# A graph attention kernel with residual norm: order of the norm pass, place of the key products, place of the list check, and an addition on GpSimd

## The chip, the core and the metric

The kernel runs on one core of one Trainium2 chip. The core has five engines with instruction queues of their own: TensorE (matrix products, PE in the profile, with its weight loads as PEld), VectorE (DVE), ScalarE (ACT), GpSimd (POOL) and SyncE (SP), which here only issues DMA transfers. They work side by side and wait for each other through semaphores. Each queue is worked off in order, so an instruction that waits holds everything behind it on its engine. The metric is the device time of one execution, in microseconds (us); lower is better.

## What is computed

A batch of 8 graphs with 2048 nodes and 64 features goes through two graph attention layers that share one adjacency matrix, then through two normalisations with a residual. Cut to what matters:

```python
h = jnp.einsum('bnc,hdc->bhnd', x, Wh)                 # four heads
out_h = _gat_layer(h, mask, bh)                         # softmax over neighbours of h.h, times h
z = leaky_relu(concat_heads(out_h), 0.2)
h2 = jnp.einsum('bnk,dk->bnd', z, Wo)
out2 = _gat_layer(h2, mask, bo)                         # the second layer, one head
z2 = leaky_relu(out2, 0.2)
out = (z2 - mean(z2)) * rsqrt(var(z2) + 1e-5) * gamma + beta
return _layernorm(x + out)                              # a second normalisation
```

`mask` is the adjacency with the diagonal set. The graph is sparse: node i and node j are joined with a probability that falls with both numbers, so the first nodes have many neighbours and the others few.

## The kernel before

The 2048 nodes are split into 56 hubs, which are treated densely, and 166 sets of 12 nodes. For each set the kernel makes a list of at most 128 nodes that any of its 12 members is joined to, gathers those rows from a table in device memory by an indirect DMA, and does attention of the 12 members against the 128 rows. The program is written in the order in which each engine is to work; nothing is reordered later.

**Lists.** The adjacency is read in pieces of 480 KB (`load_adj`, L646). SyncE issues the transfer into one of three buffers `raw`, GpSimd turns it into 0 and 1 in a tile `a` (L657) and sets the diagonal (L664). There are five buffers for `a`. `make_keys` (L689) multiplies the pieces with powers of two on TensorE (L700, tile `pk`) and packs the result with the node number into `keys` on VectorE (L685). In the first layer it has one PSUM tile, `T`, so its second half waits until VectorE has read its first half. `pick` (L710) returns a list of small VectorE jobs that take the largest keys out, eight at a time (`max` L722, `match_replace` L724), then merge them, turn them on TensorE (`slots`, L746) and build the indices and the masks. The lists come in two rounds. Round 0 (60 sets) is ready before the first layer begins. Of round 1 (106 sets) `make_keys` is called four times, k3 = 0 to 3; the first two calls lie before the first layer, the last two in it.

**First layer** (L967): a loop over 83 pairs of sets in a software pipeline. Step i issues two gathers for pair i+5, turns the rows of pair i+3 (L508), makes scores of pair i+1 (L808), masks them on VectorE (L813), takes the exponential on ScalarE (L820), multiplies by the values (L833) and divides by the sums on VectorE (`invert`, L840 and L841). Pair i goes through the head weights, and older pairs through the second projection (L867, L870) into the table of the second layer. At the end of the step come one of six pieces of the hubs (`slow`, in steps 0 to 5: turn back, heads, table, for each half of the graphs), up to two adjacency pieces (`more`), and list jobs: `some(1)` ahead of `invert`, `some(2)` behind `more`, then `make_keys` as soon as the pieces that it needs have been issued. Nine pieces are left at step 0, so these calls fall into steps 2 and 4. The 58 jobs of round 1 begin at step 5, and gathers that need round 1 begin at step 25.

**Second layer** (L1302): a loop over u, with four sets a step. A step issues gathers for step u+5 (L779, with 24 row buffers), scores for u+1 (`scores2`: L1075, exponential L1078), the value products for u (`values2`, L1103), turns of the rows for u+3 (L508, copied at L1283), the turn back of the exponentials for u+1 (L1086) and their product with the mask on VectorE (L1090). Two steps share a PSUM tile `o`, with one buffer: the even step begins it and the odd step ends it.

**Norm passes.** Behind each odd step stands the normalisation of those eight sets, number v = (u-1)/2, 21 in all, and one pass for the hubs. A pass is cut into jobs that `spread` (L1265) deals out over the following steps, and `work_on` (L1269) runs the jobs of a step at its end. Their names: `first` divides by the sums and frees `o` (L1129, L1131); `act` is the leaky slope (L1136); `mean` a sum (L1140); `centre` subtracts the mean and has ScalarE square the result (L1145, L1147); `var` sums the squares (L1152); `again` scales, multiplies by gamma, adds beta and adds the input rows `xr` (L1156, L1160, L1161, L1162); `end` scales once more and stores. `spread` appends, so the jobs of older passes in a step come before `first` of the new one. In an odd step these are either three `var` or one `again`. Every fourth step ends with a square root on ScalarE for all variances (L1274) and a reciprocal (L1275). The rows `xr` are loaded by SyncE, eight transfers a pass (L1190), and the results leave in eight transfers (L1197).

**The end.** After the last step the lists and the sums are checked against limits (L1329 to L1343): eleven small VectorE operations, a product on TensorE, and a flag that is written to device memory. Every engine then loads the flag and skips a general version of the kernel.

Of the kernel before, what the change touches and what calls it, by code (L numbers as in the profile page):

```python
# [359 lines left out]
def fast_kernel(ctx: ExitStack, tc: tile.TileContext, x, adj, Wh, bh, Wo, bo, gamma, beta, out, flag):  # L360
# [534 lines left out]
    def some(n):  # L895
        for _ in range(n):
            if picks:
                picks.pop(0)()
# [68 lines left out]
    for i in range(-3, NG + 3):  # L967
        sp = one(f"s{i}", "S")
        if 0 <= i - 3 < NG:
            second_rows(i - 3, sp[:GM, 1, 384:512])  # L970
        if 0 <= i - 2 < NG:
            second_maps(i - 2, sp[:, 0, 384:384 + GM])
        if 0 <= i + 1 < NG:
            scores(i + 1, sp)
            weigh(i + 1, sp)
        if 0 <= i < NG:
            turn_values(i, op)
            keep_values(i, op)
# [12 lines left out]
        if 0 <= i + 3 < NG:  # L991
            tp = one(f"t{i + 3}", "T")
            for j in range(2):
                turn(tp[:, j, :], rows[1, 2 * (i + 3) + j])
        if i < NG:
            cat = one(f"cat{i}", "C")
        if 0 <= i + 3 < NG + NG % 2:
            columns(i + 3, cat)
        if 0 <= i < NG:
            project(held.pop(("ot", i)), cat, GM)  # L1000
        if 0 <= i + 1 < NG:
            op = one(f"o{i + 1}", "O")
            values(i + 1, op)

        if 0 <= i - 2 < NG:
            nc.vector.tensor_copy(own[:, (i - 2) * GM:(i - 1) * GM], sp[:, 0, 384:384 + GM])
        if 0 <= i - 3 < NG:
            keep_rows(i - 3, sp[:GM, 1, 384:512])
        if 0 <= i - 1 < NG:
            leak(held["z", i - 1])  # L1010
        if 0 <= i + 3 < NG:
            t = held["T", 1, i + 3] = work.tile([P, 2, 512], F32, tag="xTg", name=f"xTg{i + 3}", bufs=3)
            nc.scalar.copy(t, tp)  # L1013
        if 0 <= i < NG:
            held["z", i] = leaky(cat, GM, f"z{i}")
        if 0 <= i + 3 < NG + NG % 2:
            keep_columns(i + 3, cat)
        if i >= 0:
            some(1)
        if 0 <= i + 1 < NG:  # L1020
            invert(i + 1, op)

        if i >= 0:
            if slow:
                slow.pop(0)()
            more(2)
            some(2)
            done = all(t // 3 > k3 for r, t, m in pieces)
            if k3 < nk and done:
                make_keys(1, k3, late_two)  # L1030
                k3 += 1
                if k3 == nk:
                    picks = pick(1)
# [82 lines left out]
    def norm(name, v, i, vals, dens, nb, xr, store):  # L1116
# [41 lines left out]
        def again():  # L1158
            scale(0)
            nc.vector.tensor_tensor(y, y, row(gam), OP.mult)  # L1160
            nc.vector.tensor_tensor(y, y, row(bet), OP.add)  # L1161
            nc.vector.tensor_tensor(y, y, xr[:, :nb], OP.add)  # L1162
# [122 lines left out]
    for w in range(-2, NB // 2 + 1):  # L1285
        if w + 2 < NB // 2:
            hub_block(w + 2)
        if w in (2, 4, 6, 7):
            for s in sets[(w - 1) // 2]:
                gather(table2, s, 2, rows2)  # L1290
        if w in (2, 4):
            spread_own(w // 2 - 1)
        if 0 <= w + 1 < NB // 2:
            hub_turn(w + 1)
        elif w + 1 < NB // 2 + 2 and w + 1 >= NB // 2:
            turn2(w + 1 - NB // 2)
        if 0 <= w < NB // 2:
            hub_scores2(w)
        if 0 <= w - 1 < NB // 2:
            hub_values2(w - 1)  # L1300
    spread(-1, norm_hub(oh2))
    for u in range(-1, NU + 12):  # L1302
        new = list(sets[u + 5]) if u + 5 < NU else []

        for s in new:
            gather(table2, s, 2, rows2)
        if u + 1 < NU:
            scores2(u + 1)
        if 0 <= u < NU:
            a = u % 2  # L1310
            if a == 0:
                op = bank2(f"o2_{u}", "O")
            values2(op, sets[u], es2[a], a, len(sets[u + 1]) if a == 0 else 0)
# [12 lines left out]
    assert not jobs  # L1326


    tot = late.tile([P, 8], F32, name="tot", bufs=1)  # L1329
    for k, r in enumerate((rall, rall2)):  # L1330
        f = r.rearrange("p g k -> p (g k)")
        nc.vector.tensor_reduce(tot[:, 2 * k:2 * k + 1], f, AX.X, OP.add)
        nc.vector.tensor_reduce(tot[:, 2 * k + 1:2 * k + 2], f, AX.X, OP.min)
        nc.vector.tensor_scalar(tot[:, 2 * k:2 * k + 1], tot[:, 2 * k:2 * k + 1], math.exp(-LOG_LOW), None, OP.is_lt)
        nc.vector.tensor_scalar(tot[:, 2 * k + 1:2 * k + 2], tot[:, 2 * k + 1:2 * k + 2], math.exp(-LOG_TOP), None, OP.is_gt)
    nc.vector.tensor_reduce(tot[:, 4:5], over, AX.X, OP.max)
    nc.vector.tensor_scalar(tot[:, 4:5], tot[:, 4:5], float(N), None, OP.is_lt)
    nc.vector.tensor_reduce(tot[:, 5:6], tot[:, 0:5], AX.X, OP.min)
    pf = bank2("pf", "T", 2)
    nc.tensor.matmul(pf[0:1, 0, 0:1], tot[:, 5:6], ones, start=True, stop=True)  # L1340
    fl = late.tile([1, 1], I32, name="fl", bufs=1)
    nc.vector.tensor_scalar(fl, pf[0:1, 0, 0:1], P - 0.5, None, OP.is_lt)
    nc.sync.dma_start(out=flag, in_=fl)  # L1343


def gat_kernel(tc: tile.TileContext, x, adj, Wh, bh, Wo, bo, gamma, beta, out):
# [36 lines left out]
```

## Time and profile before

| What | us |
|---|---|
| median of three runs | 1049.7 (1049.15 to 1050.93) |
| the profiled execution | 1191.58, mean granted clock 0.907 |
| its span, first to last instruction | 1189.8 |
| stage before the first layer | 0 to 150 |
| first layer | 150 to 728 |
| hubs of the second layer | 728 to 790 |
| second layer's loop | 790 to 1145 |
| what is left of the norm passes, and the end | 1145 to 1190 |
| busy: TensorE, VectorE, ScalarE, GpSimd | 909, 608, 536, 463 |

The profiled execution is slower than the runs without a profile, so shares and differences in it are worth more than its absolute times. The profile lists instructions by line of the code, engine and tile. In a timeline row stand the start, the duration, the engine, the line, the operation, output and inputs with their sizes, and how many were merged; in square brackets stands how long the engine had been idle before it and what ended that. A row of the costliest groups has, after the count, the busy time and the mean in ns of one, and after the second bar the idle time just before them with the releaser of most of it. "<-issue" is time in which the engine waited for nothing that the profile shows.

### The profile page before, as it was taken

How to read it: one execution, taken by the hardware profiler on the slowest of the kernel's cores; microseconds unless marked ns; L12 is line 12 of the kernel's file. 1: busy time of each engine (PE TensorE's matmuls, PEld its weight loads, DVE VectorE, ACT ScalarE, POOL GpSimd, SP SyncE). 2: the span in 40 equal slices, each digit the busy share in tenths (PEclk: the TensorE clock that was granted, in tenths of full speed). 3: DMA queues.
4: the chain of work that ended last, by engine and by line, in shares of the span. 5: the costliest groups of instructions: out<-in, count | busy, mean ns of one | idle time of the engine just before them, and what ended most of it. 6: DMA issues, size and time to landing. Idle time of an engine off the chain costs nothing.

```text
span 1189.8 us, 42920 instructions
## 1 busy us (share of the span) xinstructions
PE 909.0 (76%) x18819; PEld 734.4 (62%) x18819; DVE 608.4 (51%) x1390; ACT 536.0 (45%) x941; POOL 462.5 (39%) x669
## 2 busy tenths in 40 slices
PE   5787786788888999999999996788667676667620
PEld 4454574576767787777777775676545565555510
DVE  3378532477765444444444444123465556555685
ACT  1332352244544554545545553355544554544530
POOL 5541342333343444444445431445444444444000
PEclk9898996799999999999999998799988878888765
DMA  9775323233333333333333332755554554564111
GB/s 210 197 225 136 103 73 84 70 82 82 90 83 90 97 87 100 89 93 95 89 100 89 93 83 64 251 129 144 137 141 127 140 157 131 141 164 125 47 32 28
DMA packets 75537, 133.73 MB, mean 112 GB/s; under 512 B 29518, under 2 KB 45838, under 8 KB 75342
## 3 DMA queue, kind: packets, MB, share of 16 engines
q0 software_dynamic: 26720, 88.55, 28.2%
q1 hardware_dynamic: 31726, 38.17, 11.2%
q10 hardware_dynamic: 16896, 4.20, 2.0%
q8 instruction: 150, 2.46, 0.9%
q14 instruction: 45, 0.37, 0.1%
HBM read 118.15 MB, written 12.71 MB: 110 GB/s over the span
## 4 chain that ended last, share of the span: by engine, by line
PE 52%; DVE 24%; issue 8%; ACT 4%; another core or an unknown queue 4%; DMA 3%; POOL 2%; SPq 1%; ACTq 1%; DVEq 0%; POOLq 0%
PE o L833 12%; PE t L508 11%; PE e L1086 3%; PE cat L793 3%; PE s L808 3%; PE o L850 3%; PE o L1103 3%; DVE osb L841 3%; PE cat L527 3%; PE s L867 2%; DVE es L1090 2%; DVE var L1152 2%; DVE rall L840 2%; DVE y_s L1156 2%
## 5 line engine op out<-in xcount | busy, mean ns | idle before, releaser
L779 POOL DMA_INDIRECT g<-table,index x332 | 324.8, 978 | 258.1 <-PE o L1103 119.4
L508 PE MATMUL t<-ident,g 128*128 128x128 f32 x1328 | 201.0, 298 | 11.1 <-issue 9.1
L508 PEld LDWEIGHTS t<-ident,g 128*128 128x128 f32 x1328 | 166.3, 154 | 27.9 <-issue 22.7
L840 DVE RECIPROCAL rall<-o 64x8 f32<-64x8 f32 x166 | 34.1, 205 | 243.6 <-PE o L833 218.3
L857 ACT COPY otb<-o 128x192 f32<-128x192 f32 x166 | 44.9, 322 | 233.2 <-PE o L850 213.8
L1283 ACT COPY xTg<-t 128x1024 f32<-128x1024 f32 x83 | 82.3, 1013 | 114.1 <-PE t L508 75.5
L947 POOL COPY spot<-otb 1x1 f32<-1x1 f32 x78 | 35.1, 450 | 251.4 <-ACT otb L857 251.4
L833 PE MATMUL o<-g,e 128*64 128x65 f32 x2656 | 101.4, 225 | 16.5 <-ACT e L820 15.5
L1103 PE MATMUL o<-g,es 128*32 128x65 f32 x2656 | 60.1, 253 | 67.3 <-DVE y_s L1131 61.0
L833 PEld LDWEIGHTS o<-g,e 128*64 128x64 f32 x2656 | 88.0, 137 | 29.8 <-ACT e L820 19.4
L1090 DVE TENSOR_TENSOR es<-e,on 128x384 f32<-128x384 f32 (+1 forms) x42 | 23.2, 553 | 158.5 <-PE e L1086 115.5
L808 PE MATMUL s<-y,xTg 64*64 64x48 f32 x5248 | 102.0, 223 | 2.0 <-issue 0.8
L1103 PEld LDWEIGHTS o<-g,es 128*32 128x32 f32 x2656 | 52.2, 131 | 78.3 <-issue 67.7
L808 PEld LDWEIGHTS s<-y,xTg 64*64 64x64 f32 x5248 | 89.9, 137 | 14.3 <-issue 3.8
L820 ACT ACTIVATE e<-e,shifts 128x768 f32<-128x768 f32 x83 | 78.1, 941 | 23.6 <-DVE e L813 23.6
L813 DVE TENSOR_TENSOR e<-s,mask 128x768 f32<-128x768 f32 x82 | 78.3, 955 | 19.5 <-PE s L808 16.1
L1013 ACT COPY xTg<-t 128x1024 f32<-128x1024 f32 x83 | 83.2, 1003 | 7.6 <-PE t L508 7.6
L867 PE MATMUL s<-z,woT 128*64 128x96 f32 x664 | 68.1, 264 | 20.8 <-issue 20.6
L514 ACT ACTIVATE z<-cat,bhp 128x192 f32<-128x192 f32 x166 | 60.9, 418 | 34.1 <-PE o L833 32.6
L576 ACT ACTIVATE e<-e,shifts 128x896 f32<-128x896 f32 x32 | 33.4, 1042 | 87.1 <-DVE e L573 60.8
L867 PEld LDWEIGHTS s<-z,woT 128*64 128x64 f32 x664 | 42.9, 138 | 41.7 <-issue 28.5
L793 PE MATMUL cat<-xo,gram 128*128 128x192 f32 (+1 forms) x324 | 66.8, 329 | 0.0
(179 smaller groups left out, 1519.7 us busy)
## 6 DMA issues: line engine op xcount, KB each, us to landing
raw<-in_adj_dram SPq DMA_DIRECT2D x32, 480.0 KB
g<-table,index POOLq DMA_INDIRECT x332
table<-x SPq DMA_DIRECT2D x16, 260.0 KB
gh<-table SPq DMA_DIRECT2D x16, 260.0 KB
x<-in_x_dram ACTq DMA_DIRECT2D x32, 128.0 KB
table<-rowt SPq DMA_DIRECT2D x166, 24.4 KB
xr<-in_x_dram SPq DMA_DIRECT2D x164, 24.0 KB
out_dram<-y_s SPq DMA_DIRECT2D x164, 24.0 KB
```

The source lines that it names most:

```text
L508: nc.tensor.transpose(tp[:, q * P:(q + 1) * P], rows[:, q, 1:1 + P], ident)
L514: nc.scalar.activation(z[:, hp], cat[:, :, hp * n:(hp + 1) * n], AF.Identity, bias=bhp[:, hp:hp + 1], scale=1.0)
L779: nc.gpsimd.indirect_dma_start(out=t.rearrange("n q c -> n (q c)"), out_offset=None, in_=table, in_offset=bass.IndirectOffsetOnAxis(ap=ind ...
L793: nc.tensor.matmul(cat[:, k, 2 * GM:2 * GM + n], gram[:, g % 2 * 2 + k, :], held["x", g // 2][:, :n], start=True, stop=True)
L808: nc.tensor.matmul(sp[half(r), p, (q * 2 + j) * M:(q * 2 + j + 1) * M], xt[half(p), j, q, half(r)], y[half(p), (j * Q + q) * M:(j * Q + q ...
L813: nc.vector.tensor_tensor(e[:, :16 * M].rearrange("p (a q n) -> p a q n", a=2, q=Q), sp[:, :, :8 * M].rearrange("p a (q n) -> p a q n", q= ...
L820: nc.scalar.activation(e[:, :16 * M], e[:, :16 * M], AF.Exp, bias=shifts[:, 0:1], scale=1.0)
L833: nc.tensor.matmul(op[half(p), j, o0:o0 + K1], e[:, c0:c0 + 64], rw[:, q, sums(p)], start=True, stop=True)
L867: nc.tensor.matmul(dst, woT[:, hp, :], src, start=(hp == 0), stop=(hp == HP - 1))
L1013: nc.scalar.copy(t, tp)
L1103: nc.tensor.matmul(op[t * 32:(t + 1) * 32, f, k * W2 + p:k * W2 + p + K1], e[:, 2 * q + p, k, :], rw[:, q, sums(p)], start=(a == 0 and k = ...
L1283: nc.scalar.copy(t, tp)
```

## The change

Four edits. In the first layer `make_keys` for k3 = 2 and 3 is called at steps 6 and 8, and `some(2)` becomes `some(3)`. In the norm pass the addition of beta leaves `again`; a new job `shift`, two steps after `first`, adds beta to `xr` on GpSimd. `spread` puts `first` of a new pass ahead of the older jobs of that step, while `act` and `mean` stay behind them. The check of the limits becomes a function that is called behind the jobs of step NU - 1 = 41, the step of the last `first`, and no longer after the loop.

```diff
             more(2)
-            some(2)
-            done = all(t // 3 > k3 for r, t, m in pieces)
-            if k3 < nk and done:
+            some(3)
+            if k3 < nk and i == 6 + 2 * (k3 - 2):
+                assert all(t // 3 > k3 for r, t, m in pieces)
                 make_keys(1, k3, late_two)
                 k3 += 1
                 if k3 == nk:
...
         def again():
             scale(0)
             nc.vector.tensor_tensor(y, y, row(gam), OP.mult)
-            nc.vector.tensor_tensor(y, y, row(bet), OP.add)
             nc.vector.tensor_tensor(y, y, xr[:, :nb], OP.add)
+
+        def shift():
+            nc.gpsimd.tensor_tensor(xr[:, :nb], xr[:, :nb], row(bet), OP.add)
...
         if v % 2:
-            return [[first, act, mean(0)], [centre(0)], [], [var(0)], [], [], [again], [mean(1), centre(1)], [var(1)], [], [], [end]]
-        return [[first, act, mean(0)], [centre(0)], [var(0)], [again], [], [mean(1), centre(1)], [var(1)], [end]]
+            return [[first, act, mean(0)], [centre(0)], [shift], [var(0)], [], [], [again], [mean(1), centre(1)], [var(1)], [], [], [end]]
+        return [[first, act, mean(0)], [centre(0)], [shift, var(0)], [again], [], [mean(1), centre(1)], [var(1)], [end]]
...
     def spread(u, parts):
-        for k, part in enumerate(parts):
-            jobs.setdefault(u + k, []).extend(part)
+
+        jobs.setdefault(u, []).insert(0, parts[0][0])
+        jobs[u] += parts[0][1:]
+        for k, part in enumerate(parts[1:]):
+            jobs.setdefault(u + 1 + k, []).extend(part)
...
+    def in_limits():
+
+        tot = late.tile([P, 8], F32, name="tot", bufs=1)
...
+        nc.vector.tensor_scalar(fl, pf[0:1, 0, 0:1], P - 0.5, None, OP.is_lt)
+        nc.sync.dma_start(out=flag, in_=fl)
+
...
         work_on(u)
+        if u == NU - 1:
+            in_limits()
     assert not jobs
-
-
-    tot = late.tile([P, 8], F32, name="tot", bufs=1)
...
```

The body of `in_limits` is the code that stood at the end, unchanged.

More of the change, by code (lines that the diff above doesn't have):

```diff
@@ L1300, in fast_kernel @@
             hub_values2(w - 1)
+    def in_limits():
+        tot = late.tile([P, 8], F32, name="tot", bufs=1)
+        for k, r in enumerate((rall, rall2)):
+            f = r.rearrange("p g k -> p (g k)")
+            nc.vector.tensor_reduce(tot[:, 2 * k:2 * k + 1], f, AX.X, OP.add)
+            nc.vector.tensor_reduce(tot[:, 2 * k + 1:2 * k + 2], f, AX.X, OP.min)
+            nc.vector.tensor_scalar(tot[:, 2 * k:2 * k + 1], tot[:, 2 * k:2 * k + 1], math.exp(-LOG_LOW), None, OP.is_lt)
+            nc.vector.tensor_scalar(tot[:, 2 * k + 1:2 * k + 2], tot[:, 2 * k + 1:2 * k + 2], math.exp(-LOG_TOP), None, OP.is_gt)
+        nc.vector.tensor_reduce(tot[:, 4:5], over, AX.X, OP.max)
+        nc.vector.tensor_scalar(tot[:, 4:5], tot[:, 4:5], float(N), None, OP.is_lt)
+        nc.vector.tensor_reduce(tot[:, 5:6], tot[:, 0:5], AX.X, OP.min)
+        pf = bank2("pf", "T", 2)
+        nc.tensor.matmul(pf[0:1, 0, 0:1], tot[:, 5:6], ones, start=True, stop=True)
+        fl = late.tile([1, 1], I32, name="fl", bufs=1)
+        nc.vector.tensor_scalar(fl, pf[0:1, 0, 0:1], P - 0.5, None, OP.is_lt)
+        nc.sync.dma_start(out=flag, in_=fl)
     spread(-1, norm_hub(oh2))
@@ L1325, in fast_kernel @@
         work_on(u)
+        if u == NU - 1:
+            in_limits()
     assert not jobs
-    tot = late.tile([P, 8], F32, name="tot", bufs=1)
[L1330 to L1343, printed above, removed]
 def gat_kernel(tc: tile.TileContext, x, adj, Wh, bh, Wo, bo, gamma, beta, out):
```

## The prediction

> **What bounds the kernel now.** I read the table of engines and slices first: no engine is busy throughout (TensorE 76%, VectorE 51%), so the limit must be read stage by stage. Then the costliest groups, for what TensorE waits for:
>
> ```profile
> L779 POOL DMA_INDIRECT g<-table,index x332 | 324.8, 978 | 258.1 <-PE o L1103 119.4
> ...
> L1103 PE MATMUL o<-g,es 128*32 128x65 f32 x2656 | 60.1, 253 | 67.3 <-DVE y_s L1131 61.0
> ```
>
> The value products of the second layer (L1103) wait 61.0 us for L1131, VectorE's division by the sums, which frees their PSUM tile `o`. GpSimd's gathers wait in turn for L1103, so they follow and do not lead. The timeline shows what stands before L1131:
>
> ```profile
> 980.51 0.56 DVE L1090 TENSOR_TENSOR es<-e,on 128x384 f32<-128x384 f32 x1 [2.82 <-PE e L1086]
> 980.99 0.68 DVE L1156 TENSOR_TENSOR y_s<-y_s,var 128x512 f32<-128x512 f32 x1
> ...
> 981.70 0.69 DVE L1160 TENSOR_TENSOR y_s<-y_s,gam 128x512 f32<-128x512 f32 x1
> ...
> 982.43 0.69 DVE L1161 TENSOR_TENSOR y_s<-y_s,bet 128x512 f32<-128x512 f32 x1
> 983.15 0.69 DVE L1162 TENSOR_TENSOR y_s<-y_s,xr 128x512 f32<-128x512 f32 x1
> 983.76 0.41 DVE L1129 RECIPROCAL rall<-o 64x8 f32<-64x8 f32 x2
> 984.21 0.69 DVE L1131 TENSOR_TENSOR y_s<-o,rall 128x512 f32<-128x512 f32 x1
> ...
> 985.05 1.96 PE L1103 MATMUL o<-g,es 128*32 128x65 f32 x64 [4.15 <-DVE y_s L1131]
> ```
>
> After the mask product L1090, four operations of an older pass run (2.77 us) before the reciprocals. In this layer TensorE and VectorE hand one chain back and forth: L1090, L1131, L1103, turns L508, turns L1086, L1090. It repeats every four steps, in 35 us on the whole (L1090 at 980.51 and again at 1015.62).
>
> The first layer is bound by TensorE at 6.45 us a step (L833 from 380.96 to 568.16 in 29 steps), with two exceptions. The key products wait for GpSimd's conversion, that waits for a transfer:
>
> ```profile
> 185.26 1.09 POOL L657 TENSOR_SCALAR a<-raw 120x1024 bf16<-120x1024 int32 x1 [8.80 <-DMA raw<-in_adj_dram]
> ...
> 186.81 1.87 PE L700 MATMUL pk<-a,powers 120*32 120x512 bf16 x4 [7.33 <-POOL a L664]
> ```
>
> And where list jobs (L722, L724) run on VectorE, L833 waits for the exponential:
>
> ```profile
> 311.15 1.15 PE L833 MATMUL o<-g,e 128*64 128x65 f32 x32 [0.98 <-ACT e L820]
> ```
>
> **Sums freed first.** There are 21 such passes. From the start of L1129 to L1103 takes 1.28 us (1036.56 to 1037.84). Put first, L1103 starts 0.48+1.28 = 1.76 us after L1090's start.
>
> *Even passes* (older `again` ahead): 4.54 now (1015.62 to 1020.16), so 2.78 less. After the 4.2 us wait the granted clock is down: L1103 takes 1.96 us instead of 1.11, and L1103 to the next L1090 takes 6.8 us (1020.16 to 1026.96) against 5.2 after short waits (1003.07 to 1008.33). The wait left is about 1.4 us, so another 1.6 goes: 4.4 in each of the seven passes with waits of 4.1 to 4.3 us, 31. Two shorter ones (839.13, 1125.79) give 5.
>
> *Odd passes* (three `var`, 1.78 us): now 8.8 us from L1090 to L1090 (1034.30 to 1043.11), 10 where L1103 ran at 1.96. What is late next is ScalarE: the `var` jobs go behind `first` and end 3.4 after L1090; then square root 0.33, table 1.28, exponential 0.69, turn L1086, 1.65 to the next L1090: about 7.6. That saves 1.2 in four passes and 2.5 in the four slow ones, 15; the first and the last (823.74, 1141.30) give 2.
>
> Here a rule speaks against part of it. By the trace L1103 runs at 1.11 us after waits of 2.70 and 2.57 us, and at 1.89 to 1.96 after 2.89, 3.04 and 3.14. The Trainium skill, "TensorE: Matmul & The Clock Gate", Part 1, has the clock halved only after an idle window of some 3.4 us. By that rule the four slow odd passes are no gain of mine: 5 us less. I take the row. For the 4.2 us waits both agree.
>
> `act` and `mean` now come after the older jobs. VectorE sits idle 5.4 us before the next L1090 in the even passes (2 to 3 us remain by the sum), so this costs nothing; without that cover it would be up to 1.4 us a pass.
>
> **Shift on GpSimd.** L1161 (0.72 us start to start) leaves VectorE in 21 passes. In the even steps it stands before `centre`, whose square stands on ScalarE before the exponential that L1086 needs: on the chain, 9 x 0.72 = 6.5. In the odd steps it is already in the 2.78. In the tail, where VectorE runs without a gap, four of them: 2.9.
>
> The GpSimd add of 128x512 from two inputs has no row. Below is the memset L1058 of that size, 0.53; above is the copy L787, 0.52 for 192 columns, so 1.4 for 512. "GPSIMD Engine Reference", Performance versus the Vector engine, speaks against the move: GpSimd adds half as fast, and Specifications says that it shares its SBUF interfaces with VectorE instructions of two SBUF inputs. I take 1.2 us, by the rule and the upper row. By the rows it costs nothing: GpSimd waits 5 to 6.5 us for L1103 once in two steps. By the rule, if each held VectorE up for its whole length, 21 x 1.2 = 25. I count 0, since L1131's own inputs are not both in SBUF and VectorE idles most of the time between; 25 stays for the range.
>
> The shift is queued in order. Behind it stand the next step's four gathers, and TensorE needs those two steps later. Its own data are early: the eight transfers are issued on SyncE at 1031.4 to 1035.6, the shift is two steps (14 us) later, and the stores ahead of them are unchanged. `again` waits for it a step or more later. No wait is counted.
>
> **Key products at steps 6 and 8.** From L833 at 174.71 (step 2) to 234.79 (step 6), four steps take 60.1 us. At 6.45 they would be 25.8, and the hub's own pieces in them cost 7.2 (two table writes of about 3, the rest 0.7 each). 27 us are the two stalls and the half clock after them. All adjacency pieces are still issued in steps 0 to 4, on SyncE and GpSimd in the same order, so only TensorE is freed; the data are there long before step 6. What stays of each: six products, the wait behind L840 and L841 (2.5 us after L833), keys L685 at 1.22 and the products again, 5.1 and 4.8 us: 9.9.
>
> But the list then begins at step 9 and not 5, with four jobs a step instead of three. The step is a VectorE loop of 7.31 us (L813 at 309.18, 316.49) with two jobs of 0.92 in it; the third, `some(1)`, hides in the 1.8 us wait for L833. So 5.47 plus three: 7.76 in eight steps (each fourth job is light, 0.45), 8.23 in four, about 8 in two. Above 6.45 that is 20.8 us; now it is 10.3 (steps 6 to 25: 132.9 against 122.6). If the third job cost nothing more it would be 10. I take 20.8. Sum: -27+9.9+10.5 = **-6.6**, between -17 and +10 (the upper end if the late gathers of step 3, queued behind conversions, put the stall back). The indices are ready at step 21 as before; step 25 needs them.
>
> **The limits check.** Eleven small operations, 3.4 us (1173.91 to 1177.27), lie at the end beside 16 stores:
>
> ```profile
> 1173.41 6.46 SPq L1197 DMA_DIRECT2D out_dram<-y_s  x16
> 1179.97 0.23 SPq L1343 DMA_DIRECT2D flag<-fl  x1
> ```
>
> So they are hidden now. Moved to step 41 they stand in VectorE's gapless tail, and everything behind comes 3.4 later; the flag's issue and flight (1179.97 to its load at 1181.0) leave the end: +2.4. Bounds -1 (if gaps take them) and +4.
>
> **Sum** on the profiled execution, span 1189.8, run 1191.6: 31+5+15+2+6.5+2.9 = 62 off for the norm passes, 6.6 off in the first layer, 2.4 on: -66, or 5.5%. The median shown is 1049.7, 12% below the profiled run. In proportion that gives 991, in full 984; I take **991**, since TensorE's share of the waits is stretched by profiling.
>
> **Rivals.**
> - *GpSimd becomes the bound* (0.22). Four steps would be 29 us. Its 16 gathers at 0.98 plus 0.30, the PE releases of 0.8 to 2 us before half of them and two shifts come to 29 to 32. Then half of the norm gain is lost, 66-30 = 36: **1018**. For it: L779's releases. Against: gathers run two steps ahead.
> - *The stall stays in the first layer* (0.12), moved from L700 to gathers that sit behind the conversions: +10 instead of -6.6: **1006**.
> - *The freed wait was no limit* (0.05): L1103 finds another release and little moves, within 5 us of 1049. Against it: L1131 is the only releaser with tens of us.
> - *Slower* (0.09): the shift holds GpSimd's queue until its rows land, gathers come a step late, TensorE stands in turns L508. A hold of one step, 7 us, less about 3 of slack costs 4 in each of 21 passes, 84, against 66 saved: **1066**. It decides from about 6 us of hold. For it: one queue in order. Against it: the rows are issued 14 us ahead.
>
> **Numbers.** My forecast has 0.52. A measurement of this kernel tells 0.2% from no change (its three runs span 0.17%). Faster: 0.52+0.22+0.12+0.02 = 0.88; same 0.02; slower 0.09+0.01. The range takes in the first three with their open costs: the list's third job free and the full 66 below (968), GpSimd's bound with part of the 25 of shared access above (1028).
>
> **What would show it.** L1103's wait for L1131 falls from 61 to under 30 us; L1103 has 1.1 us throughout; four steps take 29 us. L700 no longer waits for L664. L813 repeats at 7.8 to 8.2 us in steps 9 to 22. The forecast is wrong if L508 or L1086 takes over L1103's wait, if L1162 waits for GpSimd, or if VectorE's operations beside the shift lengthen.

## The result, and the profile after

| | kernel before, us | changed kernel, us | ratio (95% interval) |
|---|---|---|---|
| first measurement, 4 runs each | 1050.3 (1049.2 to 1051.9) | 1005.3 (1001.0 to 1008.7) | 0.957 (0.953 to 0.961) |
| the same kernels on another chip | 1205.4 | 1155.1 | 0.958 (0.956 to 0.960) |

The change takes 4.3% off the time. The second row belongs here because it puts the prediction's footing right. There are chips on which the kernel before takes some 1050 us and chips on which it takes some 1200. The 1191.6 us profile of before, from which the prediction was worked out, is of the second sort, by its time and by its first-layer step of 6.45 us (below), while the times shown beside it and the profile of the changed kernel below are of the first. So absolute times are compared here only within one sort of chip. "The 1050 chips" and "the 1200 chips" stand for the two below. No chip on record was seen in both, so it cannot be told whether this lies in the chip or in a condition that it was in.

These rows of the page of the changed kernel (on a 1050 chip; its run took 1003.3 us) answer to the page rows that the prediction read:

```profile
span 1001.5 us, 43036 instructions
...
PE 806.7 (81%) x18819; PEld 680.4 (68%) x18819; DVE 613.3 (61%) x1368; ACT 528.6 (53%) x941; POOL 502.0 (50%) x691
...
L779 POOL DMA_INDIRECT g<-table,index x332 | 330.0, 994 | 135.1 <-issue 40.5
...
L1086 PE MATMUL e<-ident,eT 128*128 128x128 f32 x166 | 30.5, 312 | 58.5 <-ACT eT L1078 58.4
...
L1103 PE MATMUL o<-g,es 128*32 128x65 f32 x2656 | 54.2, 240 | 10.0 <-DVE y_s L1131 8.7
```

The wait of the value products L1103 for the division L1131 was 61.0 us and is 8.7; the two profiles come from different sorts of chip, and on a 1200 chip it is 16.6. On this 1050 chip, TensorE's largest wait in this layer is now at L1086, the turn of the exponentials, 58.4 us for ScalarE's exponential L1078. The gathers L779 still follow and do not lead: GpSimd stands 135 us before them.

The timeline of the same profile shows first a pass with its sums freed at once (828 to 834 us), then the step behind it:

```profile
828.25 0.56 DVE L1090 TENSOR_TENSOR es<-e,on 128x384 f32<-128x384 f32 x1 [1.93 <-PE e L1086]
828.73 0.41 DVE L1129 RECIPROCAL rall<-o 64x8 f32<-64x8 f32 x2
829.18 0.69 DVE L1131 TENSOR_TENSOR y_s<-o,rall 128x512 f32<-128x512 f32 x1
829.78 0.68 DVE L1156 TENSOR_TENSOR y_s<-y_s,var 128x512 f32<-128x512 f32 x1
830.01 1.75 PE L1103 MATMUL o<-g,es 128*32 128x65 f32 x64
...
834.14 0.56 DVE L1090 TENSOR_TENSOR es<-e,on 128x384 f32<-128x384 f32 x1 [0.79 <-PE e L1086]
834.62 0.68 DVE L1156 TENSOR_TENSOR y_s<-y_s,var 128x512 f32<-128x512 f32 x1
...
835.93 2.05 DVE L1145 SCALAR_TENSOR_TENSOR y_s<-st_s,y_s 128x512 f32<-128x512 f32 x1
...
836.14 1.28 POOL L1164 TENSOR_TENSOR xr<-xr,bet 128x512 f32<-128x512 f32 x1
...
841.30 0.67 ACT L1078 ACTIVATE eT<-s,shifts 128x512 f32<-128x512 f32 x1
...
842.03 1.11 PE L1086 MATMUL e<-ident,eT 128*128 128x128 f32 x4 [4.05 <-ACT eT L1078]
```

L1103 starts 1.76 us after the start of L1090 (830.01 less 828.25), as the prediction had it, and the older pass's L1156 now comes behind L1131. In the next step `centre` (L1145) takes 2.05 us, where it takes 0.69 alone: GpSimd's new addition L1164 runs beside it. Behind it stand ScalarE's squares, then the exponential, and TensorE waits 4.05 us for that.

The same timeline in the first layer, at step 6 and in the list steps:

```profile
198.77 1.47 PE L700 MATMUL pk<-a,powers 120*32 120x512 bf16 x6
...
200.28 1.22 DVE L685 SCALAR_TENSOR_TENSOR keys<-pk,number 32x1024 f32<-32x1024 f32 x1 [0.24 <-PE pk L700]
...
201.56 1.46 PE L700 MATMUL pk<-a,powers 120*32 120x512 bf16 x6 [1.31 <-DVE keys L685]
...
302.86 1.15 PE L833 MATMUL o<-g,e 128*64 128x65 f32 x32 [2.00 <-ACT e L820]
```

The key products wait for VectorE's packing alone (1.31 us) and no longer for the conversions (7.33 in the profile of before), and in the list steps L833 waits longer for the exponential: 2.00 us in this row. Compared on 1200 chips, L833 waits 15.6 us in all for it in the kernel before and 21.8 in the changed kernel.

### The profile page after: what moved, and what is told of

It reads as the page before. It is cut to its first block, busy times and chain, and to the rows that moved or that the text cites. A ratio compares the mean times of both kernels' runs of the same rounds, so it can differ in the third digit from the quotient of the medians.

```text
span 1001.5 us, 43036 instructions
## 1 busy us (share of the span) xinstructions
PE 806.7 (81%) x18819; PEld 680.4 (68%) x18819; DVE 613.3 (61%) x1368; ACT 528.6 (53%) x941; POOL 502.0 (50%) x691
## 4 chain that ended last, share of the span: by engine, by line
PE 53%; DVE 25%; issue 7%; ACT 6%; DMA 5%; POOL 2%; SPq 1%; DVEq 0%; POOLq 0%; ACTq 0%
PE o L833 10%; PE t L508 9%; PE s L808 7%; PE cat L793 4%; DMA raw<-in_adj_dram 4%; DVE y_s L1145 4%; PE o L850 4%; PE cat L527 3%; PE s L867 3%; PE e L1086 3%; PE o L1103 2%; DVE y_s L1156 2%; ACT e L820 2%; DVE es L1090 2%; ACT eT L1078 2%
## 5 line engine op out<-in xcount | busy, mean ns | idle before, releaser
L779 POOL DMA_INDIRECT g<-table,index x332 | 330.0, 994 | 135.1 <-issue 40.5
L508 PE MATMUL t<-ident,g 128*128 128x128 f32 x1328 | 171.0, 277 | 2.5 <-issue 2.1
L508 PEld LDWEIGHTS t<-ident,g 128*128 128x128 f32 x1328 | 148.7, 143 | 7.4 <-issue 3.2
L947 POOL COPY spot<-otb 1x1 f32<-1x1 f32 x78 | 41.0, 526 | 168.9 <-ACT otb L857 168.9
L833 PE MATMUL o<-g,e 128*64 128x65 f32 x2656 | 95.8, 225 | 21.4 <-ACT e L820 21.3
L813 DVE TENSOR_TENSOR e<-s,mask 128x768 f32<-128x768 f32 x82 | 78.3, 955 | 49.1 <-PE s L808 44.6
L833 PEld LDWEIGHTS o<-g,e 128*64 128x64 f32 x2656 | 84.2, 138 | 32.6 <-ACT e L820 24.9
L808 PE MATMUL s<-y,xTg 64*64 64x48 f32 x5248 | 95.8, 222 | 0.3
L1086 PE MATMUL e<-ident,eT 128*128 128x128 f32 x166 | 30.5, 312 | 58.5 <-ACT eT L1078 58.4
L1147 ACT ACTIVATE sq_s<-y_s 128x512 f32<-128x512 f32 x42 | 26.4, 630 | 85.2 <-DVE y_s L1145 77.3
L657 POOL TENSOR_SCALAR a<-raw 120x1024 bf16<-120x1024 int32 (+1 forms) x34 | 38.2, 1127 | 65.5 <-DMA raw<-in_adj_dram 40.1
L1090 DVE TENSOR_TENSOR es<-e,on 128x384 f32<-128x384 f32 (+1 forms) x42 | 23.2, 553 | 71.0 <-PE e L1086 70.5
L1086 PEld LDWEIGHTS e<-ident,eT 128*128 128x128 f32 x166 | 20.6, 156 | 64.8 <-ACT eT L1078 64.8
L1103 PE MATMUL o<-g,es 128*32 128x65 f32 x2656 | 54.2, 240 | 10.0 <-DVE y_s L1131 8.7
```

Source lines behind the costliest of these rows:

```text
L508: nc.tensor.transpose(tp[:, q * P:(q + 1) * P], rows[:, q, 1:1 + P], ident)
L779: nc.gpsimd.indirect_dma_start(out=t.rearrange("n q c -> n (q c)"), out_offset=None, in_=table, in_offset=bass.IndirectOffsetOnAxis(ap=ind ...
L808: nc.tensor.matmul(sp[half(r), p, (q * 2 + j) * M:(q * 2 + j + 1) * M], xt[half(p), j, q, half(r)], y[half(p), (j * Q + q) * M:(j * Q + q ...
L813: nc.vector.tensor_tensor(e[:, :16 * M].rearrange("p (a q n) -> p a q n", a=2, q=Q), sp[:, :, :8 * M].rearrange("p a (q n) -> p a q n", q= ...
L833: nc.tensor.matmul(op[half(p), j, o0:o0 + K1], e[:, c0:c0 + 64], rw[:, q, sums(p)], start=True, stop=True)
L1086: nc.tensor.transpose(te[:, k, :], e[:, k, :], ident)
```

## Experiments

All runs but no_limits met 1200 chips. "Before" is the kernel before, run on the same chip beside it:

| run | what differs from the changed kernel | us | before, us | ratio (95%) |
|---|---|---|---|---|
| no_first | older jobs ahead of `first` again | 1190.2 | 1205.6 | 0.984 (0.979 to 0.990) |
| no_keys | key products in steps 2 and 4 and three list jobs a step again | 1162.8 | 1205.6 | 0.964 (0.960 to 0.968) |
| no_shift | beta added on VectorE again | 1155.2 | 1205.6 | 0.959 (0.953 to 0.964) |
| no_shift_b | the same | 1159.0 | 1205.4 | 0.960 (0.956 to 0.963) |
| no_shift_c | the same | 1160.4 | 1205.3 | 0.964 (0.960 to 0.968) |
| after_again | nothing | 1155.1 | 1205.4 | 0.958 (0.956 to 0.960) |
| one_input | beta on VectorE, an idle one-input operation on GpSimd | 1149.9 | 1205.4 | 0.954 (0.951 to 0.956) |
| ns_keys67 | beta on VectorE, key products at steps 6 and 7, three list jobs a step | 1147.1 | 1205.4 | 0.954 (0.949 to 0.959) |
| ns_keys67_b | the same | 1135.3 | 1191.1 | 0.952 (0.948 to 0.956) |
| ns_keys67_c | the same | 1148.7 | 1204.1 | 0.952 (0.948 to 0.956) |
| no_limits | list check at the end again (a 1050 chip) | 1011.7 | 1054.3 | 0.957 (0.951 to 0.963) |

What each stage took was read from the timelines, from the starts of VectorE's L813 (one a step in the first layer) and of L1090 (one a step in the second). The second layer's steps come in four kinds, named by the VectorE work behind their L1090: A frees the sums of an even pass, B has two means and centres, C frees those of an odd pass and has three `var`, D has `again` and `centre`. The A to D columns are means without the first two of a kind. The tail runs from the last L1090 to the end. All in us:

| profile | first layer, steps 0-5 | 5-9 | 9-25 | second layer's loop | A | B | C | D | tail |
|---|---|---|---|---|---|---|---|---|---|
| before_again | 63.1 | 31.1 | 112.6 | 357.1 | 11.05 | 7.59 | 9.30 | 7.86 | 46.0 |
| after_again | 36.6 | 38.7 | 124.7 | 318.2 | 7.97 | 7.90 | 7.66 | 7.92 | 40.4 |
| no_first | 40.6 | 42.3 | 124.7 | 351.4 | 10.27 | 7.84 | 9.37 | 7.64 | 40.3 |
| no_keys | 61.4 | 31.1 | 112.6 | 316.8 | 8.01 | 7.97 | 7.52 | 7.87 | 40.4 |
| no_shift_b | 38.0 | 38.0 | 125.1 | 317.3 | 7.92 | 7.58 | 7.69 | 7.95 | 43.0 |
| one_input | 37.1 | 38.9 | 125.0 | 309.3 | 8.08 | 7.75 | 7.51 | 7.30 | 43.0 |
| ns_keys67 | 36.4 | 40.3 | 114.0 | 315.8 | 7.87 | 7.64 | 7.62 | 7.95 | 42.8 |
| after (1050 chip) | 33.9 | 33.6 | 112.0 | 268.0 | 5.45 | 8.80 | 6.46 | 6.86 | 39.8 |
| no_limits (1050 chip) | 34.3 | 32.5 | 110.1 | 268.5 | 5.72 | 8.58 | 6.45 | 6.89 | 43.7 |

**Is it the profiling, or the chip?** The kernel before, unchanged, profiled once more.

> The kernel before, unchanged, for a second profile. The profiled execution of before took 1191.6 us against a median of 1049.7, that of the changed kernel 1003.3 against 1005.3, so the two traces stand on different footings. Expected: a span near 1048, a step of the first layer outside the list jobs at 5.4 to 5.5 us (5.44 in the changed kernel's trace) and not 6.45, with L1103 still waiting some 60 us for L1131. If the step is 6.45 again, the change itself would have shortened it, which no part of the prediction says.

It took 1206.8 us with its profile, and the unprofiled runs beside it a median of 1205.6. So a profiled execution is as long as the others on its chip, and the statement that it is slower, on which the scaling in the prediction rested, was wrong; that the first profile of before came from a 1200 chip follows from its 1191.6 us. Nor did the expected 5.4 us for a first-layer step come: it is 6.56 in before_again and 6.57 in the changed kernel on a 1200 chip (after_again), so the change does not shorten it. What sets the chips apart is shown by the changed kernel in one stretch of the first layer. The columns are the window, its length, then busy time and number of records of PE, PEld, DVE, ACT and POOL, the granted clock, the DMA share and GB/s. On the 1050 chip:

```profile
420.00:560.00 140.00, 139.87 (x3492) 121.55 (x3492) 74.07 (x180) 87.61 (x182) 77.89 (x117) 1.00 0.42 110
```

And after_again on a 1200 chip:

```profile
420.00:560.00 140.00, 128.41 (x2900) 108.18 (x2904) 62.27 (x151) 73.51 (x151) 62.82 (x96) 1.00 0.34 90
```

At the same full clock the second does 17% fewer matrix products in the same time. Its timeline shows how, at each step:

```profile
463.19 0.70 PE L867 MATMUL s<-z,woT 128*64 128x96 f32 x6
464.22 0.33 PE L867 MATMUL s<-z,woT 128*64 128x96 f32 x2 [0.34 <-issue]
```

TensorE stands between two products of one line, waiting for nothing that the profile shows. A first-layer step takes 6.57 us there and 5.45 on the 1050 chip. Most of this is at the one line L867, the second projection: between 460 and 560 us it has 13.8 us busy and 6.9 us of such gaps for 120 products there, against 10.2 us and no gaps for 146 products on the 1050 chip. With eight of them in a step that is some 0.8 of the 1.1 us. Why these chips issue later was not found.

**Sums first.** The diff against the changed kernel:

```diff
-        jobs.setdefault(u, []).insert(0, parts[0][0])
-        jobs[u] += parts[0][1:]
-        for k, part in enumerate(parts[1:]):
-            jobs.setdefault(u + 1 + k, []).extend(part)
+        for k, part in enumerate(parts):
+            jobs.setdefault(u + k, []).extend(part)
```

> The changed kernel with the jobs of older passes ahead of first again. Prediction: the order is worth 53 us of the profiled execution, in proportion 47, so about 1052. Rival (even steps bound by the exponential take back half): about 1028. L1103 should wait some 50 us for L1131 again.

Measured 1190.2 us, 35 more than after_again (another chip, with before at 1205.6 and 1205.4). The page of no_first has the old wait back:

```profile
L1103 PE MATMUL o<-g,es 128*32 128x65 f32 x2656 | 61.4, 257 | 58.3 <-DVE y_s L1131 51.4
```

The second layer's loop grows from 318.2 to 351.4 us, all of it in steps A (7.97 to 10.27) and C (7.66 to 9.37); B and D do not grow. This edit carries about two thirds of the 50 us. In ratios, the expectation was 1.00 by the prediction and 0.98 by the rival; 0.984 lies nearer to the rival. The rival's reason, that the exponential bounds the even steps, is not shown by that: TensorE waits 16.1 us in all for the exponential in after_again.

**Key products.** The diff:

```diff
-            some(3)
-            if k3 < nk and i == 6 + 2 * (k3 - 2):
+            some(2)
+            done = all(t // 3 > k3 for r, t, m in pieces)
+            if k3 < nk and done:
```

> The changed kernel with the key products as early as their data are issued (steps 2 and 4) and three list jobs a step. Prediction: the move is worth 6.6 us, so about 1012. Rival 1 (four jobs a step on VectorE's loop cost as much as the stall): 1005, the same. Rival 2 (the stall of 27 us at full speed is worth 15 or more): 1020.

Measured 1162.8, 7.7 more than after_again on its other chip, about what the prediction had. The timeline of no_keys has the stalls on the conversions back:

```profile
191.66 1.86 PE L700 MATMUL pk<-a,powers 120*32 120x512 bf16 x4 [7.54 <-POOL a L664]
...
217.25 1.44 PE L700 MATMUL pk<-a,powers 72*32 72x512 bf16 x3 [5.49 <-POOL a L664]
```

Steps 0 to 5 take 61.4 us instead of 36.6, steps 5 to 9 7.6 less and steps 9 to 25 12.1 less. Most of the freed stall is given back by the key products themselves and by the fourth list job a step.

**The shift on GpSimd.** The diff, run three times on three chips:

```diff
             nc.vector.tensor_tensor(y, y, row(gam), OP.mult)
+            nc.vector.tensor_tensor(y, y, row(bet), OP.add)
             nc.vector.tensor_tensor(y, y, xr[:, :nb], OP.add)
-        def shift():
-            nc.gpsimd.tensor_tensor(xr[:, :nb], xr[:, :nb], row(bet), OP.add)
```

> The changed kernel with the addition of beta back on VectorE. Theory A (the prediction: the shift is free on GpSimd, the addition costs 0.72 us on the chain nine times and in the tail four times): 9 us slower, about 1014. Theory B (the shift holds VectorE up: L1156 x2 takes 2.91 us instead of 1.28 beside it, and L1145 2.05 instead of 0.69, about 1.4 us in each of 20 passes, in the even steps whose chain ends at the exponential): 28 off, 7 on, about 985; L1156 at 0.69 throughout and L1086's wait for the exponential down by some 20 us.

> The changed kernel, unchanged, beside the three that follow. The last four ran on a chip on which the kernel before takes 1206 us and TensorE stands in 'issue' more often, and the changed kernel was not among them. Expected: 0.957 of the kernel before on a chip where that takes 1050 us; on the slower one 0.955 to 0.965. The shift beside VectorE again at L1156 or L1145 of 2 to 2.9 us.

> The addition of beta back on VectorE, now directly beside the changed kernel. Theory A (prediction: the shift saves 9 us): 0.9% slower than the changed kernel. Theory B (it costs 1.4 us a pass in the even steps' chain, 28, and saves 7): 2% faster on a chip of 1050 us. On the slower chip, where its steps show more of other waits and GpSimd runs the shift at another moment, half of that.

> The kernel without the shift once more, in the hope of a chip on which the kernel before takes 1050 us. There four steps of the changed kernel's second layer took 27.6 us, of which the two with a shift beside VectorE 8.8 and 6.9; on the slower chips all four take 7.7 to 8.0 with or without the shift. Theory: where TensorE is fast, VectorE's chain is the bound and the shift costs 15 to 20 us: 0.94 of the kernel before. Rival: it costs nothing there either: 0.957 to 0.963.

The ratios without the shift are 0.959, 0.960 and 0.964, and with it 0.958: on 1200 chips the move is worth between nothing and 0.6%. Of that the tail shows 2.8 us (43.7, 43.0 and 42.9 us without, 40.4 with). The loop shows nothing: 314.3, 317.3 and 315.3 us without, 318.2 with. The timeline of after_again shows why the 0.7 us taken from VectorE in a pass do not come out:

```profile
935.98 1.11 PE L1103 MATMUL o<-g,es 128*32 128x65 f32 x64 [1.25 <-DVE y_s L1131]
...
938.88 0.60 PE L1086 MATMUL e<-ident,eT 128*128 128x128 f32 x4
...
942.71 0.56 DVE L1090 TENSOR_TENSOR es<-e,on 128x384 f32<-128x384 f32 x1 [3.40 <-remote]
...
958.70 1.28 POOL L1164 TENSOR_TENSOR xr<-xr,bet 128x512 f32<-128x512 f32 x1
958.86 2.28 DVE L1156 TENSOR_TENSOR y_s<-y_s,var 128x512 f32<-128x512 f32 x2
```

In the first three rows VectorE is idle for 3.40 us before L1090, so time saved on it is not time saved in the step. In the last two, the two L1156 take 2.28 us beside the shift; no_shift has the same pair at 1.28. In the loop and tail of after_again eight operations of VectorE are stretched so, by 7.2 us together; in the changed kernel on the 1050 chip it is twelve, by 17.3 us (against the durations of the same forms alone); in no_shift none. In after_again little of it reaches the step: of the steps D from 9 to 29, those with a stretched pair take 7.84 to 7.98 us and those without one 7.80 to 7.84.

On the 1050 chip it is otherwise, and the trace of the changed kernel shows it by two of its own steps D. VectorE does the same work in both. In the first the shift L1164 comes behind `centre` (L1145), in the second beside it:

```profile
765.62 0.56 DVE L1090 TENSOR_TENSOR es<-e,on 128x384 f32<-128x384 f32 x1 [1.48 <-PE e L1086]
...
768.80 0.68 DVE L1145 SCALAR_TENSOR_TENSOR y_s<-st_s,y_s 128x512 f32<-128x512 f32 x1
769.40 1.65 DVE L1089 TENSOR_SCALAR on<-mask 128x48 f32<-128x48 uint8 x1
...
769.71 1.28 POOL L1164 TENSOR_TENSOR xr<-xr,bet 128x512 f32<-128x512 f32 x1
...
770.78 0.66 PE L1086 MATMUL e<-ident,eT 128*128 128x128 f32 x4 [1.31 <-ACT eT L1078]
...
771.47 0.56 DVE L1090 TENSOR_TENSOR es<-e,on 128x384 f32<-128x384 f32 x1 [0.42 <-PE e L1086]
...
907.34 0.56 DVE L1090 TENSOR_TENSOR es<-e,on 128x384 f32<-128x384 f32 x1 [1.49 <-PE e L1086]
...
910.52 1.97 DVE L1145 SCALAR_TENSOR_TENSOR y_s<-st_s,y_s 128x512 f32<-128x512 f32 x1
910.66 1.27 POOL L1164 TENSOR_TENSOR xr<-xr,bet 128x512 f32<-128x512 f32 x1
...
913.78 1.12 PE L1086 MATMUL e<-ident,eT 128*128 128x128 f32 x4 [2.62 <-ACT eT L1078]
...
914.94 0.56 DVE L1090 TENSOR_TENSOR es<-e,on 128x384 f32<-128x384 f32 x1 [2.35 <-PE e L1086]
```

The first step takes 5.85 us, the second 7.60. The stretched `centre` delays the exponential, and L1086 starts 6.44 us after L1090 and not 5.16. L1086 then takes 1.12 us, at a granted clock of 0.50, and not 0.66 at 1.00. The five steps D with a stretched operation take 7.3 to 7.6 us and the others with the same list of operations 5.85 or 5.86. Six steps B take 8.9 to 9.4, against 6.95 in the one with the same list and nothing stretched, whose first operation is smaller by 0.26. The trace of no_limits, also from a 1050 chip, shows the same. Estimated from these steps, the stretching costs 5 x 1.6 + 6 x 2.0 = 20 us on that chip, 2% of the time. These are steps of one trace beside each other; a kernel without the shift was not run on a 1050 chip.

Which operations are stretched can be read from the same trace. The twelve read two SBUF tiles. The division L1131, which reads PSUM, keeps its 0.69 us where the shift lies beside it (735.55, the shift from 734.73). But the small conversion L1089, with one input, takes 1.65 us instead of 0.17 beside the shift in the rows above. So two inputs are not the only case.

To see whether the second input matters, beta went back to VectorE and GpSimd got an operation on a tile of its own with one input:

```diff
+            nc.vector.tensor_tensor(y, y, row(bet), OP.add)
...
-        def shift():
-            nc.gpsimd.tensor_tensor(xr[:, :nb], xr[:, :nb], row(bet), OP.add)
+        def idle():
+            nc.gpsimd.tensor_scalar(junk, junk, 1.0, None, OP.mult)
```

> The addition of beta on VectorE, and in the place of the shift a GpSimd operation of the same size with one input on a tile of its own (it changes no result). If VectorE is held by any GpSimd operation of this length, or if what costs is GpSimd's own queue, L1156 and L1145 stretch as they do beside the shift and the time is that of the changed kernel plus 7 us. If it is the second input that collides, they stay at 0.69 and the time is that of the kernel without the shift.

The timeline of one_input, whose lines are shifted by two:

```profile
859.09 1.51 POOL L1167 TENSOR_SCALAR junk<-junk 128x512 f32<-128x512 f32 x1
859.23 1.64 DVE L1158 TENSOR_TENSOR y_s<-y_s,var 128x512 f32<-128x512 f32 x2
```

The same pair takes 1.64 us: stretched by 0.36 instead of 1.00, though GpSimd is busy for longer. Nine operations are stretched, by 3.4 us in all, where the shift stretched eight by 7.2. So a one-input operation of GpSimd holds VectorE up too, but less. The two operations differ in kind as well as in the second input, so the price is not shown to be the second input's alone. The time did not come out as either side of the expectation had it. That this kernel, with an idle operation added, ran at 0.954 beside 0.960 for no_shift_b is not explained: its loop is 8 us shorter, nearly all of it in steps D. Differences of half a per cent between arrangements of this layer on these chips are therefore not put down to a cause here.

**The list check.** The diff:

```diff
         work_on(u)
-        if u == NU - 1:
-            in_limits()
     assert not jobs
+    in_limits()
```

> The changed kernel with the check of the lists behind the loop again, where it was. Prediction: the check in VectorE's gapless tail costs 3.4 us and the flag at the end 1.0, so without the move the time is 2.4 us less; the part behind the last L1090 38 us instead of 40.4. Rival: the tail of the changed kernel is 5.6 us shorter than before (46.0 to 40.4), of which the kernel without the shift accounts for 2.9 only, so the move has saved the other 2.7: 43 us, and the time 2.7 us more.

The ratio is 0.957, as with the check moved, with an interval that would hide half a per cent. The tail tells more: 43.7 us against 39.8. The last rows of the timeline of the changed kernel, whose span ends at 1001.5:

```profile
990.81 1.29 DVE L1156 TENSOR_TENSOR y_s<-y_s,var 128x512 f32<-128x512 f32 x2
991.53 6.93 SPq L1199 DMA_DIRECT2D out_dram<-y_s  x16
```

And those of no_limits, whose span ends at 1011.8:

```profile
995.92 6.12 SPq L1199 DMA_DIRECT2D out_dram<-y_s  x15
...
1002.15 0.23 SPq L1322 DMA_DIRECT2D flag<-fl  x1
```

From the last store's issue (991.53 + 6.93) to the end are 3.0 us in the first, and from the flag's issue to the end 9.7 in the second. So the rival of the expectation was right about the tail. With the check moved the flag leaves at 973.07, and its flight and the engines' loads of it lie beside the rest of the tail.

**A better arrangement.** Without the shift, and with the second group of key products a step earlier, so that three jobs a step are enough:

```diff
-            some(3)
-            if k3 < nk and i == 6 + 2 * (k3 - 2):
+            some(2)
+            if k3 < nk and i == 6 + (k3 - 2):
...
+            nc.vector.tensor_tensor(y, y, row(bet), OP.add)
...
-            nc.gpsimd.tensor_tensor(xr[:, :nb], xr[:, :nb], row(bet), OP.add)
```

> Without the shift, and with the key products at steps 6 and 7 and three list jobs a step from step 8 (20 steps) in the place of steps 6 and 8 and four jobs from step 9 (15 steps). By the loop of VectorE (5.2 us and about 0.8 for each job behind invert, TensorE 5.44): three jobs 6.9 us, four jobs 7.1 to 7.5; excess 20 x 1.4 = 28 against 15 x 1.8 = 27. Theory: no more than 3 us from the kernel without the shift. Rival (four jobs a step are too many): 8 us faster.

> No shift, key products at steps 6 and 7, three list jobs a step. Its trace keeps the two parts apart: the first layer shows the list jobs, the four steps between the mask products L1090 of the second layer show the shift. On a slow chip as before: 0.954. On a chip of 1050 us, theory (VectorE is the bound there): the steps that hold the shift fall from 8.8 to about 7.4 and from 6.9 to 6.2, 20 us in all; steps 5 to 25 as long as in the changed kernel within 5; about 983, 0.936. Rival (the shift is harmless there too): the steps as in the changed kernel, 0.957.

> The same kernel as ns_keys67: the shift undone (bet added on VectorE again), the key groups at steps 6 and 7 with three jobs a step; norm order and limits check as in the change. Which chip it gets decides what it can tell: on one where the kernel before takes some 1050 us the shift can be priced, where it takes some 1200 us it can't. Theory (the shift stretches VectorE's two-input operations, and where a first-layer step takes 5.43 us the second layer is bound by the chain through VectorE and ScalarE, so the stretching is paid): the second-layer steps that held the shift fall from 8.8 to 7.3-7.8 and from 6.9 to 6.2-6.6 us, the span between the first and the last second-layer step from 268 to 250-260, first-layer steps 0 to 25 stay at 177-182, the tail is 43; ratio to the kernel before 0.935-0.950. Rival (the chain there is hidden behind other waits): these two kinds of step stay within 0.2 us of 8.8 and 6.9, the bet add returns 6 us to VectorE; ratio 0.955-0.962. On a slower chip both expect 0.952-0.954 and nothing is told.

0.954, 0.952 and 0.952: with one_input's 0.954 the lowest of all, each below the changed kernel's 0.958. On the one chip that ran both it is 1147.1 against 1155.1 us, with intervals that overlap a little. Steps 9 to 25 take 114.0 us instead of 124.7, so it is the list jobs that gain; the missing shift neither helps nor harms there. Against no_shift_b, on the same chip, ns_keys67 is 11.9 us faster: the rival of its expectation (8 us) was right and the theory (no more than 3) was not. All three runs met 1200 chips, so for the shift on a 1050 chip there is only the estimate of 20 us above.

## Why the prediction was right, and where it was not

The forecast of 991 us was 14 below the 1005.3 measured, with the measured time in its range and on the right side. On its own footing, from one profiled 1200 chip to another, it said -66 us of 1191.6, and before_again to after_again gives -52 (1205.0 to 1153.0 in span):

| stage | predicted | measured |
|---|---|---|
| first layer, keys | -6.6 | -6.8 |
| second layer's loop: sums first | -53 | -41.5 |
| second layer's loop: beta and shift | -6.5 | +2.6 |
| tail: beta | -2.9 | -2.8 |
| tail: check | +2.4 | -2.8 |

The loop's two rows part 357.1 to 318.2 at the mean of the three no_shift profiles, 315.6; the tail's part 46.0 to 40.4 at their 43.2. How the loop is parted depends on the order in which the edits are taken. With beta off VectorE but the old order (no_first) the loop is 351.4: beta then gives -5.7 and the order -33.2. The two edits overlap, since L1161 was one of the four operations ahead of the division and no longer stands there once the division goes first.

**The bound was read rightly.** L1103's wait for L1131 was the limit: undoing that edit alone brings back 51.4 us of wait and 35 us of time. It fell to 8.7 us, and to 16.6 on the 1200 chip.

**Sums first: the mechanism right, the even passes too large.** Odd passes were to gain 17 us, 1.7 in each of ten; C fell by 1.6. Even passes were to gain 36, 4.0 in each of nine; A fell by 3.1, and all steps A together by 27.0 (to the mean of the three no_shift profiles). That is 9 of the 11.5 us missing; most of the rest is in steps B, which grew by 1.8 together. The mis-sized term is the 1.6 us for the clock, by which L1103 to the next L1090 was to fall from 6.8 to about 5.2. In those seven passes it is 6.9 us in before_again and still 6.6 in after_again. The clock did come back: L1103 takes 1.11 us in five of the seven. But in the pass shown (935.98 to 942.71) L1090 starts 3.2 us after L1086 has ended (938.88 + 0.60), with gaps of issue on TensorE between; why it starts so late is not shown. On the 1050 chip the stretch takes 4.1 (830.01 to 834.14).

The prediction also read from its rows that L1103 runs at half clock after a wait of 2.89 us or more and at the full one after 2.70 or less. No such line holds. L1103 took 1.96 us after a wait of 2.57 in before_again (849.01) and 1.11 after 2.85 in no_first (991.62). In the profile of before itself it took 1.96 after 1.71 (966.24), where the granted clock had been 0.50 since 960.80, before that wait began. The 3.4 us that the prediction set against its rows are no line for the wait just before L1103 either: half clock followed 2.57. After the change, L1103 does not run at 1.1 us throughout: it takes 1.75 in the first timeline above.

**The shift counted at nothing: wrong.** The prediction set aside the rule of the Trainium skill, "GPSIMD Engine Reference", Specifications, on the shared SBUF interfaces, because L1131's inputs are not both in SBUF and VectorE idles much. About L1131 it was right: it is not lengthened. But the shift meets L1156, L1145 and L1161 as well, which read two SBUF tiles, and adds 0.5 to 1.7 us to each of the twelve (1050 chip) or eight (1200 chip) that were stretched. The rule was right for these and the duration too (1.28 us measured, 1.2 estimated); L1089, with one input, shows that two inputs, as the prediction gave the rule, are not all. The 6.5 us gain in the loop did not come on top of the new order, since VectorE had idle time before L1090 in those steps. On 1200 chips this cost 9 us of the forecast as the table parts it, as far as single profiles tell. On the 1050 chip the stretched operations stand ahead of the exponential that TensorE waits for, and cost 20 us by the estimate above. The upper price that the prediction named and set aside, 25 us, is near to that.

**The keys: right in every term, within 2.3 us.** -26.5, +7.6 and +12.1 measured (63.1 to 36.6, 31.1 to 38.7, 112.6 to 124.7), against -27, +9.9 and +10.5. A list step takes 7.8 us on the 1200 chip, as forecast, and 7.0 on the 1050 chip.

**The check: the wrong sign.** The 3.4 us on VectorE were priced; the way from the flag's issue to the end was taken as 1.03 us, from issue to the load, and is 9.7. The prediction's own rows had it: the flag is issued at 1179.97 and the span ends at 1189.8, 9.8 us later. Leaving it beside the tail pays for the move and 2.8 us more.

**What is late next.** Two of the three signs that the prediction named against itself came: VectorE's operations beside the shift lengthen, and on the 1050 chip L1086 takes over the wait. The forecast of the time held all the same. On the 1050 chip L1086 stands 58.4 us for the exponential, which comes behind ScalarE's squares, which wait for VectorE's `centre`. Whether that was so before the change can't be told, as there is no profile of the kernel before from such a chip; on 1200 chips L1086's wait for L1078 is 15.4 and 12.1 us in the two profiles of before and 16.1 after. Four steps take 31.5 us there (29 forecast) and 27.6 on the 1050 chip.

**The rivals.** GpSimd did not become the bound (it still stands 135 us, 203 on the 1200 chip, before its gathers), the stall on the conversions is gone, and nothing on the trace waited for L1164, so the slower case had no start.

**The scale.** 991 was taken in proportion, for the wrong reason (profiling instead of another chip). The ratios on the two sorts of chip agree, 0.957 and 0.958; but the way there differs (A takes 5.45 us on the one and 7.97 on the other), and the shift costs 20 us by estimate on the one and nearly nothing on the other. So the agreement is measured and not explained, and that a forecast from the one sort came out on the other was luck as far as the record shows.

## What to carry to other kernels

Free the PSUM tile first and let older work follow: putting two small operations ahead of others in one engine's queue gave 35 of 50 us here. Before an addition is moved to GpSimd, look which VectorE operations will run beside it: those with two SBUF inputs paid for it here, up to the length of the addition itself and beyond. Then look whether VectorE stands idle afterwards: where it did (the 1200 chips) the price did not show in the step, and where its work led to the next wait (the 1050 chip) it did. And compare a profile with times only after making sure that both come from the same sort of chip, with the duration of one repeated step as the mark.

## What was not expected of the hardware

- The same program takes 1050 us on some chips and 1190 to 1205 on others. In the stretch of the first layer that was compared, the granted clock is 1.00 on both, and most of the difference is at one line (L867), with gaps of 0.3 to 0.7 us between products that no wait explains.
- GpSimd's two-input addition of 128x512, 1.28 us, lengthens a two-input VectorE operation of that size beside it by up to 1.7 us (`centre`, L1145, from 0.69 to 2.43); a one-input one of 1.51 us lengthens a pair of such operations by 0.36. The division L1131, which reads PSUM, was not lengthened.
- From the issue of a four-byte flag as the last transfer to the end of the span pass 9.7 us; from the issue of the last store, 3.0.
